# Sparse graph attention: 72 gathered chunks in place of 75 per sweep, and the second block's first rows fetched earlier

## The chip, the cores and the metric

The kernel runs on one core of a Trainium2 chip. The metric is the device time of one execution in microseconds, from the first to the last instruction. The profile is of one such execution.

## The reference

Four layers are applied to `x` of shape (16 graphs, 1024 nodes, 128 features), all with the same adjacency matrix `adj` (1024 x 1024, an entry is 1 with probability 1/128, so a node has about eight neighbours). Layers L0, L2 and L3 are attention layers with eight heads of 16; L1 is a graph attention layer. Cut to what matters:

```
def attention_layer(adj, h):                       # L0, L2, L3
    Q, K, V = h @ Wq, h @ Wk, h @ Wv               # 8 heads of 16
    s = einsum('bnhd,bmhd->bhnm', Q, K) / sqrt(16)
    a = softmax(where(adj == 0, -inf, s))          # over neighbours m
    x = layer_norm(h + einsum('bhnm,bmhd->bnhd', a, V) @ Wo + bo)
    return layer_norm(x + relu(x @ W1 + b1) @ W2 + b2)

def graph_layer(x, adj):                           # L1
    h = x @ W
    e = leaky_relu((h @ a_src)[:, :, None] + (h @ a_dst)[:, None, :])
    att = nan_to_num(softmax(where(adj == 0, -inf, e)))
    return layer_norm(att @ h + x)
```

All is in float32.

## The kernel before

**Sorting and slots.** `graph` counts each node's neighbours, ranks the nodes by degree, and cuts the ranking into 32 row groups of 32 nodes (T = 8 sorted rows of 128 nodes, J = 4 groups in each). A destination tile t is made of four groups j, one from each group column; `row_of(t, j)` says from which sorted row the group comes. `CAPS` says how many neighbours a group may have. For each sorted row, in the order `order`, the kernel fetches the adjacency rows by an indirect DMA (`by_position`) and finds the neighbours by rounds of max-of-eight and match-replace on DVE (L370 to L378). `slots` then makes, for each tile, the lists of neighbours (`idx`) and the 0/1 matrices (`marks`).

**Chunks.** A chunk (j, r) holds four slots (S = 4) for each of the 32 nodes of group j, so it fills 128 partitions. One indirect DMA on POOL's queue (L908) gathers the 128 rows of a chunk from a table of keys and values in DRAM. What remains over whole chunks of four is put together in one mixed chunk per tile (`MIX`), which serves two of the groups in halves of 64 partitions (`SHARED`). The chunks of a tile are cut into pieces of one or two (`PIECES`). With the mixed chunks there are 75 chunks in the eight tiles.

**Units and parts.** The 16 graphs are taken in two halves (`GR`, g). A unit is (layer, half, tile), so there are 64 units, eight for each half of each layer; these eight are called a sweep here, or a block in the title. The main loop runs over parts. In an attention layer a part is one piece; in L1 up to two pieces are one part. For a part, `products` (L920, DVE) multiplies the gathered keys with the queries, `exponentials` reduces them (L943, DVE) and takes the exponential (L947, ACT), `weighted` (L971, DVE) multiplies the values, and `summed` (L987, PE) sums over the slots by matmuls of `marks`, 32 output columns each, the output going to the PSUM partitions of group j. `gathered(i - 1 + AHEAD)` issues the gathers four parts ahead, into a ring of four buffers. In L1 there are no products with queries. `divided` closes a unit (the reciprocal at L1024).

**What lies between.** The order of instructions on every engine is written out by hand. Each part has three turns `others()` (four in L1), in which generators advance one step: the `tails` of the unit before (output projection, two layer norms, the feed-forward part, the projection for the next layer's tables, L543 to L731), then the first of `fronts` (slots of the next unit, input rows, weights, queries), then `loads`, then `slow`. `slow` is `at_leisure(1)`: during the first sweep of L0 it makes the tables of the second half of the graphs, in 16 steps of transposes (L617) and projections (L547). Before the first gather of the second sweep (u == T in `gathered`), all of `slow` that is left is advanced to its end. `loaded(u)` fetches the input rows of L0's units by indirect DMAs on POOL's queue (L827), in two halves h, and turns each with PE transposes (L617). [...]

Of the kernel before, what the change touches and what calls it, by code (L numbers as in the profile page):

```python
# [16 lines left out]
I32 = mybir.dt.int32  # L17
# [33 lines left out]

S = 4
J = P // 32
CAPS = (24, 14, 14) + 5 * (12,) + 8 * (10,) + 8 * (8,) + 6 * (6,) + 2 * (4,)
TOP = max(CAPS)
QUADS = TOP // S
MIX = J

def row_of(t, j):
    return T - 1 - t if j % 2 else t


def cap(t, j):
    return CAPS[row_of(t, j) * J + j]


COUNT = [[cap(t, j) // S for j in range(J)] for t in range(T)]  # L70

SHARED = [[j for j in range(J) if cap(t, j) % S] for t in range(T)]
assert all(len(_s) == 2 for _s in SHARED) and all(c % (S // 2) == 0 for c in CAPS)

PIECES = []
for _t in range(T):
    PIECES.append([])
    for _r in range(max(COUNT[_t])):
        for _p in range(2):
            _c = [(_j, _r) for _j in (_p, _p + 2) if COUNT[_t][_j] > _r]  # L80
            _last = PIECES[_t][-1] if PIECES[_t] else []
            if len(_c) == len(_last) == 1 and _c[0][0] == _last[0][0]:
                _last.extend(_c)
            elif _c:
                PIECES[_t].append(_c)
    PIECES[_t].insert(3, [(MIX, 0)])

PLACE = {
# [5 lines left out]
for _t in range(T):  # L94
    for _j in range(J):
        for _r in range(COUNT[_t][_j]):
            MARK[_t, _j, _r] = len(MARK)
    for _k in range(2):
        MARK[_t, MIX, _k] = len(MARK)


def of_piece(v, piece):
# [25 lines left out]
def sparse_path(ctx: ExitStack, tc: tile.TileContext, a: dict, out: bass.AP, flag):  # L128
# [87 lines left out]
    def graph(wide):  # L216
# [18 lines left out]
        nc.gpsimd.memset(lists, 0.0)  # L235
        for e in wide[3:] + wide[:1] + wide[2:3]:
            nc.gpsimd.memset(e, 0.0)
        caps = s1.tile([P, T], F32, name="caps")
        cols = s1.tile([P, 2, T], F32, name="cols")
        nid = s1.tile([P, T], F32, name="nid")  # L240

# [53 lines left out]
            yield 1  # L295

        rank_i = s1.tile([P, T], I32, name="rank_i")
        flip = s1.tile([P, T], I32, name="flip")
        nc.vector.tensor_copy(rank_i, rank)
        nc.vector.tensor_scalar(flip, rank_i, 32, None, ALU.bitwise_and)  # L300
        nc.vector.tensor_scalar(flip, flip, float((T - 1) * P // 32), None, ALU.mult)
        nc.vector.tensor_tensor(flip, rank_i, flip, ALU.bitwise_xor)
        where = s1.tile([P, T], F32, name="where")
        nc.vector.tensor_copy(where, flip)

        pack = s1.tile([P, T], F32, name="pack")
        nc.vector.tensor_scalar(pack, nid, -1.0, float(2 * N * N + N), ALU.mult, ALU.add)
# [34 lines left out]
                in_offset=bass.IndirectOffsetOnAxis(ap=node_i[:, q : q + 1], axis=0),  # L342
            ))

        order = [q for k in range(T // 2) for q in (k, T - 1 - k)]
        ahead = [by_position(q) for q in order[:3]]
        there = s1.tile([P, T], F32, name="there")
        for j in range(J):
            rows = slice(32 * j, 32 * j + 32)
            if j % 2 == 0:  # L350
                nc.vector.tensor_copy(there[rows], node[rows])
                continue
            for t in range(T):
                q = row_of(t, j)
                nc.vector.tensor_copy(there[rows, t : t + 1], node[rows, q : q + 1])
# [4 lines left out]
                    ALU.mult, ALU.add,  # L360
                )
        low = s1.tile([P, T], F32, name="low")
        nc.vector.tensor_tensor(bad, sorted_[:, :, 2], caps, ALU.is_gt)
        nc.vector.tensor_scalar(low, sorted_[:, :, 2], 1.0, None, ALU.is_lt)
        nc.vector.tensor_tensor(bad, bad, low, ALU.add)
        yield 2
# [1 line left out]
        for at, q in enumerate(order):  # L368
            v = vs[:, :N]
            nc.vector.scalar_tensor_tensor(v, ahead[at], 0.0, values, ALU.not_equal, ALU.mult)  # L370
            if at + 3 < T:
                ahead.append(by_position(order[at + 3]))
            top = -(-CAPS[q * J] // 8) * 8
            for k in range(0, top, 8):
                nc.vector.max(lists[:, q, k : k + 8], v)
                if k + 8 < top:
                    last, v = v, vs[:, N:] if k % 16 == 0 else vs[:, :N]
                    nc.vector.match_replace(v, lists[:, q, k : k + 8], last, 0.0)  # L378
                yield 1
            if 0 < at < 5:  # L380
                yield ("spread", "load", "slots", "queries")[at - 1]

    def slots():

        def spread(q):
            ps = bank([P, J, TOP])
            for j in range(J):
                nc.tensor.matmul(
                    ps[:, j, :], rep_of(j, True), lists[:, row_of(q, j), :],
                    start=True, stop=True,  # L390
                )
            return ps

        for q in range(T):
            ps = spread(q)
            yield
            if q:
                yield
            for s in range(S):
                at = slice(32 * s, 32 * s + 32)  # L400
                nc.vector.tensor_copy(
                    val[at], ps[at].rearrange("p j (k s) -> p j k s", s=S)[:, :, :, s]
                )

            first, second = SHARED[q]
            for k in range(2):
                at = slice(32 * (2 + k), 32 * (3 + k))
                to, of = COUNT[q][first], S * COUNT[q][second] + k
                nc.vector.tensor_copy(val[at, first, to : to + 1], ps[at, second, of : of + 1])

            def flat(v):
                return v.rearrange("p j k -> p (j k)")

            nc.vector.tensor_copy(flat(val_i), flat(val))

            for k, (by, op) in enumerate(
                ((2 * N - 1, ALU.bitwise_and), (11, ALU.logical_shift_right))
            ):
                nc.vector.tensor_scalar(flat(part), flat(val_i), by, None, op)
                nc.vector.tensor_scalar(  # L420
                    flat(idx[:, k, q]), flat(part), -1.0, float(N), ALU.mult, ALU.add
                )
            nc.vector.tensor_scalar(flat(used), flat(val), 0.0, None, ALU.is_gt)
            for j in range(J):
                c, n = MARK[q, j, 0], COUNT[q][j]
                nc.vector.tensor_tensor(
                    marks[:, c : c + n, :],
                    used[:, j, :n].rearrange("p (k o) -> p k o", o=1).to_broadcast([P, n, 32]),
                    mark32.to_broadcast([P, n, 32]),
                    ALU.mult,  # L430
                )
            for k in range(2):
                at, r = slice(64 * k, 64 * k + 64), COUNT[q][first]
                nc.vector.tensor_tensor(
                    marks[at, MARK[q, MIX, k], :],
                    used[at, first, r : r + 1].to_broadcast([64, 32]),
                    mark32[at, 0, :],
                    ALU.mult,
                )
            yield  # L440
# [410 lines left out]
    def queries(u):  # L851

        l, g, t = units[u]
        if not is_attention(u):
            ps = bank([P, J + 1, G])
            for j in range(J):
                nc.tensor.matmul(ps[:, j, :], rep_of(j, True), srcs[g, t], start=True, stop=True)
            for k, j in enumerate(SHARED[t]):
                at = slice(64 * k, 64 * k + 64)
                nc.tensor.matmul(  # L860
                    ps[at, MIX, :], rep_of(j, True)[:, at], srcs[g, t], start=True, stop=True
                )
            ofs[u] = smalls.tile([P, J + 1, G], F32, tag="of", name="of")
            nc.scalar.copy(ofs[u], ps)
            return
# [20 lines left out]
    def shared(u):  # L886

        qx[u] = queries_of_shared()
        for k, j in enumerate(SHARED[units[u][2]]):
            at = slice(64 * k, 64 * k + 64)  # L890
            nc.sync.dma_start(qx[u][at], qs[u][at, j, :])

    def gathered(i):
        if i >= len(parts):
# [1 line left out]
        u, pieces = parts[i]  # L896
        if u == T:
            while slow:
                advance(slow)
        l, g, t = units[u]  # L900
        width = tables[l, g].shape[1]
# [78 lines left out]
    def marked(t, chunk, outs, rhss):  # L980

        j, r = chunk
        for mark, j in (
            [(MARK[t, j, r], j)] if j < J else [(MARK[t, MIX, k], SHARED[t][k]) for k in range(2)]
        ):
            mine = [c for c in sum(PIECES[t], []) if c[0] == j or c[0] == MIX and j in SHARED[t]]
            nc.tensor.matmul(  # L987
                outs[32 * j : 32 * j + 32], marks[:, mark, :], rhss,
                start=(chunk == mine[0]), stop=(chunk == mine[-1]),
            )  # L990

    def summed(i):
# [3 lines left out]
        r = pieces[-1][-1][1]  # L996
        if is_attention(u) and i + 1 < len(parts) and pieces[-1][-1][0] != MIX:
            v, ((first, *_), *_) = parts[i + 1]
            if v == u and first[1] == r and first[0] != MIX:
                return  # L1000
        if u not in accums:
            accums[u] = accs.tile([P, HF, GH * D], F32, tag="acc", name="acc")
# [75 lines left out]
    with tc.manual_schedule():  # L1078
# [27 lines left out]
        prods = ctx.enter_context(tc.tile_pool(name="prods", bufs=4))  # L1106
        smalls = ctx.enter_context(tc.tile_pool(name="smalls", bufs=3))
        slow.append(at_leisure(1))
        for i in range(AHEAD - 1):
            gathered(i)  # L1110
        nc.gpsimd.memset(wide[3], 0.0)
        gathered(AHEAD - 1)
        fronts.extend([islice(rest, 3), loaded(1)] + more)
        closing, sizes = None, ()
        begun = 0
        for i in range(len(parts) + 2):
# [499 lines left out]
```

## Time and profile before

| what | value |
|---|---|
| median of 3 runs | 2327.65 us |
| lowest, highest | 2319.72, 2335.47 us |
| span of the profiled execution | 2318.9 us |
| PE busy | 2064.1 us (89%) |
| DVE busy | 1933.8 us (83%) |
| ACT busy | 1528.7 us (66%) |
| POOL busy | 1091.8 us (47%) |
| mean granted PE clock | 0.955 |
| moved by DMA | 636.05 MB |

A busy share is an average over stages with different limits. In what follows the span is cut at the reciprocals of L1024, one per unit, and each stretch is read by itself. In a row of the table of groups, the two numbers after the first bar are the busy time and the mean duration of one (ns), and after the second bar stands how long the engine was idle just before, with what ended most of it. In a timeline line the first number is the start, the second the time, both in us.

### The profile page before, as it was taken

How to read it: one execution, taken by the hardware profiler on the slowest of the kernel's cores; microseconds unless marked ns; L12 is line 12 of the kernel's file. 1: busy time of each engine (PE TensorE's matmuls, PEld its weight loads, DVE VectorE, ACT ScalarE, POOL GpSimd, SP SyncE). 2: the span in 40 equal slices, each digit the busy share in tenths (PEclk: the TensorE clock that was granted, in tenths of full speed). 3: DMA queues.
4: the chain of work that ended last, by engine and by line, in shares of the span. 5: the costliest groups of instructions: out<-in, count | busy, mean ns of one | idle time of the engine just before them, and what ended most of it. 6: DMA issues, size and time to landing. Idle time of an engine off the chain costs nothing. (4 is left out here: it accounts for less than half of the span.)

```text
span 2318.9 us, 36591 instructions
## 1 busy us (share of the span) xinstructions
PE 2064.1 (89%) x13124; PEld 1274.2 (55%) x13124; DVE 1933.8 (83%) x1486; ACT 1528.7 (66%) x5057; POOL 1091.8 (47%) x754
## 2 busy tenths in 40 slices
PE   7469999889998999997999989999999989898987
PEld 6326666555555555554565655655555555455554
DVE  7978788698889577778888899988898888988893
ACT  3227777767776655565576776787776767676764
POOL 3444435345454578883343434343354544544441
PEclk8779999999999999999899999999999999999988
DMA  7767878778787799997987978888887777676760
GB/s 265 243 232 259 291 275 284 273 249 294 267 295 267 235 329 354 345 367 268 326 289 275 320 269 290 285 316 290 284 282 272 255 268 281 231 270 242 269 246 21
DMA packets 168461, 636.05 MB, mean 274 GB/s; under 512 B 38328, under 2 KB 41144, under 8 KB 119774
## 3 DMA queue, kind: packets, MB, share of 16 engines
q0 software_dynamic: 92672, 485.09, 58.4%
q1 hardware_dynamic: 75600, 148.55, 19.0%
q8 instruction: 105, 1.72, 0.3%
q14 instruction: 84, 0.69, 0.1%
HBM read 603.11 MB, written 92.34 MB: 300 GB/s over the span
## 5 line engine op out<-in xcount | busy, mean ns | idle before, releaser
L908 POOL DMA_INDIRECT e<-table,idx x600 | 880.5, 1468 | 1029.6 <-DVE pr L971 834.7
L971 DVE TENSOR_TENSOR pr<-e,ex 128x2048 f32<-128x2048 f32 (+1 forms) x336 | 689.2, 2060 | 21.8 <-ACT ex L959 16.1
L920 DVE TENSOR_TENSOR pr<-e,qr 128x2048 f32<-128x2048 f32 x204 | 461.8, 2264 | 160.5 <-DMA e<-table,idx 88.9
L987 PE MATMUL acc<-pr,marks 128*32 128x512 f32 x2656 | 537.0, 615 | 38.2 <-DVE pr L971 28.3
L943 DVE TENSOR_REDUCE sc<-pr 128x128 f32<-128x2048 f32 (+1 forms) x252 | 518.5, 2058 | 8.6
L595 ACT ACTIVATE z<-yps,root 128x128 f32<-128x128 f32 x888 | 316.9, 387 | 35.7 <-PE yps L710 18.8
L987 PEld LDWEIGHTS acc<-pr,marks 128*32 128x32 f32 x2656 | 109.3, 111 | 291.1 <-issue 219.4
L706 PE MATMUL yps<-W,f 128*128 128x128 f32 x1520 | 251.7, 282 | 7.4 <-ACT f L701 0.7
L610 ACT ACTIVATE z<-yps,rstd 128x128 f32<-128x128 f32 x888 | 253.4, 368 | 7.2
L701 ACT ACTIVATE f<-ps,b 128x512 f32<-128x512 f32 x190 | 130.8, 692 | 157.4 <-PE ps L692 153.9
L706 PEld LDWEIGHTS yps<-W,f 128*128 128x128 f32 x1520 | 204.5, 191 | 48.8 <-issue 26.5
L547 PE MATMUL ps<-Wkv,xT 128*128 128x256 f32 x768 | 218.0, 426 | 12.7 <-ACT xT L623 4.3
L880 PE MATMUL ps<-q,rep 32*128 32x512 f32 x768 | 179.0, 656 | 47.3 <-ACT q L875 44.9
L883 ACT COPY qr<-ps 128x512 f32<-128x512 f32 x384 | 197.0, 599 | 31.7 <-PE ps L880 30.9
L947 ACT ACTIVATE ex<-sc 128x128 f32<-128x128 f32 (+1 forms) x252 | 78.6, 312 | 194.7 <-DVE sc L943 194.5
L617 PE MATMUL ps<-ident,z 128*128 128x128 f32 x896 | 175.6, 299 | 34.8 <-ACT z L610 29.9
L617 PEld LDWEIGHTS ps<-ident,z 128*128 128x128 f32 x896 | 114.6, 142 | 158.7 <-ACT z L610 85.8
L595 ACT ACTIVATION_READ_ACCUMULATOR z<-yps,root 128x1 f32 x888 | 201.3, 227 | 0.0
L551 ACT COPY kv<-ps 128x512 f32<-128x512 f32 x176 | 103.0, 590 | 136.7 <-PE ps L547 109.4
L547 PEld LDWEIGHTS ps<-Wkv,xT 128*128 128x128 f32 x768 | 149.8, 209 | 70.4 <-ACT qr L883 19.8
L692 PE MATMUL ps<-x,W 128*128 128x512 f32 x384 | 187.1, 610 | 0.9 <-ACT x L625 0.9
L681 PE MATMUL yps<-Wo,oT 128*128 128x128 f32 x768 | 159.2, 290 | 10.0 <-ACT oT L623 10.0
(173 smaller groups left out, 2724.3 us busy)
## 6 DMA issues: line engine op xcount, KB each, us to landing
table<-kv SPq DMA_DIRECT2D x88, 512.0 KB
qx<-qr SPq DMA_DIRECT2D x96, 256.0 KB
kept<-xT SPq DMA_DIRECT2D x96, 256.0 KB
x<-kept SPq DMA_DIRECT2D x48, 512.0 KB
e<-table,idx POOLq DMA_INDIRECT x600
table<-kv SPq DMA_DIRECT2D x32, 256.0 KB
edges<-in_adj SPq DMA_DIRECT2D x8, 512.0 KB
spare<-in_x SPq DMA_DIRECT2D x8, 512.0 KB
```

Of the source, the lines that this page charges most:

```text
L547: nc.tensor.matmul(ps[:, k, :], x[:, i + k, :], w[LAYERS[l][0], "Wkv"], start=True, stop=True,)
L595: nc.scalar.activation(z[:, i, :], y[:, i, :], AF.Square, scale=D**-0.5, bias=root, accum_out=total[:, i : i + 1],)
L610: nc.scalar.activation(z[:, i, :], y[:, i, :], AF.Copy, scale=rstd[:, i : i + 1])
L617: nc.tensor.transpose(ps[:, i, :], z[:, i, :], ident)
L692: nc.tensor.matmul(ps, p["W1"][:, f * P : (f + 1) * P], x1.rearrange("p g n -> p (g n)"), start=True, stop=True,)
L706: nc.tensor.matmul(ps[:, i, :], f1[:, f, i * P : (i + 1) * P], p["W2"][:, f, :], start=(f == 0), stop=False,)
L883: nc.scalar.copy(qs[u][:, j, h * GH * D : (h + 1) * GH * D], pss[j])
L908: nc.gpsimd.indirect_dma_start(out=es[i][:, k, :], out_offset=None, in_=tables[l, g][:, :], in_offset=bass.IndirectOffsetOnAxis(ap=idx[:, ...
L920: nc.vector.tensor_tensor(prs[i][0][:, :n, :], es[i][:, :n, :ROW], qx[u].rearrange("p (o c) -> p o c", o=1) if (MIX, 0) in piece else of_p ...
L943: nc.vector.tensor_reduce(sc[:, :n, :], prs[i][0][:, :n, :].rearrange("p k (a d) -> p k a d", d=HD), mybir.AxisListType.X, ALU.add,)
L971: nc.vector.tensor_tensor(prs[i][k0 // 2][:, :m, :].rearrange("p k (a d) -> p k a d", d=d), es[i][:, k0 : k0 + m, base : base + ROW].rearr ...
L987: nc.tensor.matmul(outs[32 * j : 32 * j + 32], marks[:, mark, :], rhss, start=(chunk == mine[0]), stop=(chunk == mine[-1]),)
```

## The change

Slots are counted in ones. `CAPS` and `row_of` become hand-set tables: for each tile four capacities, and for each group column the order of the sorted rows. What is over in each group, now 0 to 3 slots, fills quarters of 32 partitions of the mixed chunk (`QUARTERS`), so that up to three groups share it. The pieces are made by taking the chunks two at a time. There are 72 chunks: tile 0 has 11 in place of 12, tile 7 has 7 in place of 9, the others have 9 as before. In `graph`, a node's place is looked up from its rank by a compare with 32 group numbers and a sum of `MOVES`, in place of a bit flip; the rows are searched in another order, and the steps of the first slots, the loading and the first queries are yielded in another order. `shared` copies quarters. In `gathered`, when `slow` is driven to its end before the second sweep, tails that hold buffers are advanced first. In `summed`, no more than two parts are summed together. Last, the generator `loaded(1)` is started before the first gathers, so that its first fetch of rows stands ahead of them on POOL's queue.

```diff
-CAPS = (24, 14, 14) + 5 * (12,) + 8 * (10,) + 8 * (8,) + 6 * (6,) + 2 * (4,)
+ROWS = (
+    (0, 1, 2, 3, 4, 5, 7, 6),
+    (7, 6, 3, 5, 2, 1, 0, 4),
+    (7, 6, 5, 1, 2, 0, 3, 4),
+    (1, 0, 2, 3, 4, 7, 5, 6),
+)
+CAPS = (
+    (24, 5, 4, 11), (12, 6, 6, 12), (10, 9, 8, 9), (9, 8, 11, 8),
+    (8, 10, 10, 8), (7, 12, 13, 4), (5, 14, 9, 8), (6, 8, 8, 6),
+)
...
 PIECES = []
 for _t in range(T):
-    PIECES.append([])
-    for _r in range(max(COUNT[_t])):
-        for _p in range(2):
...
+    _c = [(_j, _r) for _r in range(QUADS) for _j in (0, 2, 1, 3) if COUNT[_t][_j] > _r]
+    PIECES.append([sorted(_c[_k : _k + 2]) for _k in range(0, len(_c), 2)])
     PIECES[_t].insert(3, [(MIX, 0)])
...
-        nc.vector.tensor_scalar(flip, rank_i, 32, None, ALU.bitwise_and)
-        nc.vector.tensor_scalar(flip, flip, float((T - 1) * P // 32), None, ALU.mult)
-        nc.vector.tensor_tensor(flip, rank_i, flip, ALU.bitwise_xor)
+        nc.vector.tensor_scalar(rank_i, rank_i, 5, None, ALU.logical_shift_right)
+        nc.vector.tensor_copy(ranks, rank_i)
+        which = junk[:, : T * T * J].rearrange("p (t k) -> p t k", t=T)
+        nc.vector.tensor_tensor(
+            which,
+            ranks.rearrange("p (t o) -> p t o", o=1).to_broadcast([P, T, T * J]),
+            iota[:, : T * J].rearrange("p (o k) -> p o k", o=1).to_broadcast([P, T, T * J]),
+            ALU.is_equal,
+        )
...
-        order = [q for k in range(T // 2) for q in (k, T - 1 - k)]
+        order = sorted({row_of(0, j) for j in range(J)})
+        order += [q for q in range(T) if q not in order]
...
             if 0 < at < 5:
-                yield ("spread", "load", "slots", "queries")[at - 1]
+                yield ("load", "spread", "queries", "slots")[at - 1]
...
         if u == T:
             while slow:
+                while busy[0] and not held[0]:
+                    advance(tails)
                 advance(slow)
...
-            if v == u and first[1] == r and first[0] != MIX:
+            if v == u and first[1] == r and first[0] != MIX and i - 1 not in prs:
                 return
...
         slow.append(at_leisure(1))
+        second = loaded(1)
+        next(second)
         for i in range(AHEAD - 1):
             gathered(i)
         nc.gpsimd.memset(wide[3], 0.0)
         gathered(AHEAD - 1)
-        fronts.extend([islice(rest, 3), loaded(1)] + more)
+        fronts.extend([islice(rest, 3), second] + more)
```

## The prediction

> **What bounds the kernel now.** First the totals, then the table of operation groups, then the stretches between the reciprocals at L1024. There is one reciprocal per unit (eight destination tiles of a layer and half of the graphs), so a stretch between two of them is about one unit.
>
> ```profile
> PE 2064.1 (89%) x13124; PEld 1274.2 (55%) x13124; DVE 1933.8 (83%) x1486; ACT 1528.7 (66%) x5057; POOL 1091.8 (47%) x754
> ```
> PE and DVE are both nearly full; over the whole span neither stands out as the bound.
>
> ```profile
> L908 POOL DMA_INDIRECT e<-table,idx x600 | 880.5, 1468 | 1029.6 <-DVE pr L971 834.7
> L987 PE MATMUL acc<-pr,marks 128*32 128x512 f32 x2656 | 537.0, 615 | 38.2 <-DVE pr L971 28.3
> L943 DVE TENSOR_REDUCE sc<-pr 128x128 f32<-128x2048 f32 x198 | 452.6, 2286 | 6.8
> L943 DVE TENSOR_REDUCE sc<-pr 128x64 f32<-128x1024 f32 x54 | 65.9, 1220 | 1.8
> L971 DVE TENSOR_TENSOR pr<-e,ex 128x1024 f32<-128x1024 f32 x72 | 87.9, 1221 | 2.9 <-issue 2.9
> L920 DVE TENSOR_TENSOR pr<-e,qr 128x2048 f32<-128x2048 f32 x198 | 454.4, 2295 | 160.5 <-DMA e<-table,idx 88.9 <-PE acc L987 46.1 <-issue 8.0
> ```
> In an attention layer a piece of two chunks costs DVE 2.295 + 2.286 + 2.288 = 6.87 us (product, reduce, weighting); a piece of one chunk costs 1.22 × 3 = 3.66 us. The gathers are no bound: POOL mostly waits for DVE to free a buffer.
>
> The stretches, in order: two of the first block (layer L0, first half of the graphs), an ordinary unit of L2, a unit 0 of L2, and an L1 unit 0 with the unit after it. Columns: length; busy PE, PEld, DVE, ACT, POOL; PE clock; DMA.
>
> ```profile
> core 0: us, PE busy (x) PEld busy (x) DVE busy (x) ACT busy (x) POOL busy (x), PEclk, DMA share, GB/s
> 213.20:254.90 41.70, 39.44 (x263) 26.03 (x260) 35.46 (x37) 31.13 (x104) 16.92 (x12) 1.00 0.78 275
> 420.00:465.90 45.90, 39.64 (x264) 26.14 (x262) 32.39 (x18) 32.63 (x111) 15.25 (x10) 1.00 0.69 250
> 1233.30:1269.70 36.40, 34.08 (x223) 21.57 (x223) 32.16 (x19) 27.63 (x89) 14.31 (x10) 1.00 0.87 296
> 1379.80:1423.40 43.60, 38.56 (x242) 22.61 (x244) 42.45 (x26) 28.99 (x92) 19.51 (x13) 1.00 0.75 261
> 923.10:945.60 22.50, 21.63 (x133) 11.18 (x131) 16.31 (x22) 10.63 (x41) 18.98 (x14) 1.00 0.88 291
> 945.60:964.20 18.60, 16.47 (x127) 10.09 (x126) 12.62 (x18) 10.26 (x40) 15.68 (x12) 1.00 0.98 364
> ```
> The limits differ by unit. Unit 0 (12 chunks) is bound by DVE: 42.45 of 43.60 us. An ordinary unit of 9 chunks has PE at 34.08 and DVE at 32.16 of 36.40; both have a few microseconds of slack. L0's first block is bound by PE (39.44 of 41.70), because it also projects the other half of the graphs. L1's units move data almost all the time (DMA share 0.98).
>
> **The first unit**, by the timeline from the first gather on:
>
> ```profile
> 84.85 1.18 POOL L908 DMA_INDIRECT e<-table,idx  x1 [3.47 <-issue]
> 97.25 2.29 DVE L920 TENSOR_TENSOR pr<-e,qr 128x2048 f32<-128x2048 f32 x1 [3.35 <-DMA e<-table,idx]
> 100.72 0.96 POOL L827 DMA_INDIRECT rows<-in_x,places  x1 [0.30 <-issue]
> 108.75 1.09 PE L617 MATMUL ps<-ident,rows 128*128 128x128 f32 x4 [20.29 <-DMA rows<-in_x,places]
> 116.66 2.89 POOL L827 DMA_INDIRECT rows<-in_x,places  x1 [0.30 <-issue]
> 125.89 1.09 PE L617 MATMUL ps<-ident,rows 128*128 128x128 f32 x4 [3.49 <-DMA rows<-in_x,places]
> 159.65 0.77 DVE L401 COPY little<-ps 32x24 f32<-32x24 f32 x4 [8.20 <-PE ps L388]
> ```
> PE stood 20.29 us for the first half of unit 1's input rows, which POOL issued after seven gathers. But DVE works nearly throughout: between 97.25 and the reciprocal at 169.8 it is busy 60.4 of 72.5 us, and its own waits there are 3.4 (first gather), 2.7 (L493 for PE L488) and 8.2 (L401 for PE L388). Those 14.3 us are all that a better start could give DVE.
>
> [...] 2656 records of 615 ns are 1633 us of durations in 537 us of busy time, a factor of 3.0. [...] Here PE got the rows 8.0 us after their issue (100.72 to 108.75)[...].
>
> **Part 1: three chunks fewer.** By the slot tables unit 0 goes from 12 to 11 chunks (seven pieces to six; a one-chunk piece goes) and unit 7 from 9 to 7 (five pieces to four; a two-chunk piece goes). Units 1 to 6 keep nine chunks. This happens in 2 halves × 4 layers. DVE work removed in the six attention sweeps: 6 × (3.66 + 6.87) = 63.2 us, and two weightings in each of L1's two sweeps, 2 × (2.29 + 1.22) = 7.0: together 70.2 us. How much of it shows:
> - Unit 0, attention. DVE-bound, so all 3.6 us count: 38.8 us of DVE remain, above PE (38.56 less one chunk). A chunk on PE is (38.56 − 34.08)/3 = 1.49 us. Five such units outside the first block: −18.0. Bounds per unit: 2.5 to 3.7.
> - Unit 7, attention. DVE falls to 25.3 us and stops counting. PE falls by 2 × 1.49 to 31.1; with the 2.4 us of PE idle kept, 36.4 becomes 33.5: −3.0. Bounds: 0 (the chain of its tail sets it) and 4.8 (PE leaves 0.6 us idle). Four such units: −12.0. The very last unit has the same piece less ahead of its end: −3.5 (0 to 6.9).
> - L1: (22.50 − about 17.4 for the units around)/3 = 1.7 us a chunk, as DMA and PE share the bound; three chunks, two sweeps, give 10; I take −8, because the units next to the layer's ends overlap attention work.
> - Marks. Units 2 and 6 now share their mixed chunk among three row groups, not two: one more mark matmul each (L987 falls only from 1328 to 1312 matmuls). [...] 0 to 1.49 us a unit, taken as 0.25; 16 units: +4.
> - Queries of the mixed chunk go in 108 copies rather than 96, with the same bytes: SP adds 12 issues of about 0.55 us on an engine that waits most of the time; nothing. ACT loses 12 exponentials, POOL 24 gathers; both hidden, since neither is a bound.
>
> **Part 2: the start.**
> - The map from rank to place: five operations of 0.2 us become three such, two of 256 elements (nearest row, L451 128x256, 0.42), a reduce (L449, 0.41) and an add: about 2.0 against 1.0, +1.0 on the path. The 14 additional one-column copies at 0.07 lie under the 3.5 us wait for the first gathered edges.
> - Unit 0's slots need five searched rows (0, 1, 7, 2, 3) and not four: six more operations of 1.24 us, so the indices are ready at 77.4 + 1.0 + 7.5 = 85.9. The first gather started at 84.85, held by the table's writes, so it moves by about +1.5. The search as a whole has the same 26 operations.
> - The first half's rows of unit 1 now go out while POOL waits for those indices: the issue costs nothing, and the 20.29 us wait is gone.
> - The second half's rows still follow the gathers that wait for the first weighting. Before, that weighting ended at 112.0 and PE had the rows at 125.9. PE now meets this transpose ahead of the first sums (eight L987 matmuls, 3.6 us) and of L488, for which DVE's L493 waits. Rows at about 127.4, L488 done at about 133; DVE is ready at about 124.4: a wait of 8.6 in place of 2.7, +5.9. In exchange L388 no longer sits behind a row transpose: −8.2. With unit 0's piece: 1.5 + 5.9 − 8.2 − 3.7 = −4.5.
> - Unit 0 has one piece and so three filler turns fewer, so unit 2's two halves are turned back to back in unit 1. PE waits for the second, again behind gathers: 4 to 10 us, less what such waits cost there before; taken as +5.
> - One projection step of the other half moves from unit 0 to unit 7, where all that is left is forced out before the second block's first gather: 1.1 + 3.8 = 4.9 us of PE in a PE-bound stretch, against −3.0 for its two chunks: +2.
> - Sum of the first block: +2.5; bounds −11 and +15.
>
> **Sum:** −18.0 − 12.0 − 3.5 − 8 + 4 + 2.5 = −35.0 us on the span of 2318.9, hence 2283.9. The three runs have a median of 2327.65, 8.7 above that span; so 2292.6, taken as 2292. About 1% (23 us) is what a measurement of this kernel can tell from no change.
>
> **The rivals.**
> - *DVE sets the time throughout.* All 70.2 us count and the start gives its 11 us: 2327.65 − 81 = 2246. For it: DVE at 88% even in ordinary units, and POOL's 834.7 us of waiting for DVE. Against: PE at 34.08 of 36.40 in those units. Chance 0.15.
> - *Unit 7 gives nothing*, since its tail steps and the next queries, which have to fit in four pieces, become the chain. Then −18.0 − 3.4 (L1's unit 0) + 4 + 2.5 = −15: 2313. For it: ordinary units take 36.4 with either engine short of full. Chance 0.22.
> - *PE's granted clock falls.* It is 0.955 in the mean, with stretches at 0.91 where PE is at 36.3 of 36.4 us. If denser PE work lowers it, each 0.01 costs 2064 × 0.01/0.955 = 21.6 us; from 0.016 on the gain is gone, and 0.03 would give 2327.65 − 35 + 65 = 2358. Against: the stretches at 0.91 took no longer than the others, so not every dip reaches the end. Chance 0.10.
> - That the change doesn't do what it says is excluded by the instruction order: 576 gathers against 600, and one row fetch ahead of them.
>
> **How the numbers follow.** The forecast has 0.53; its own range is 2268 to 2312. Faster by over 1% (under 2304): 0.44 of the forecast, all 0.15 of the first rival, 0.04 of the second, 0.63. Within 1%: 0.09 + 0.17 + 0.01 = 0.27. Slower: 0.10. The range runs from the middle of the first rival to above the second, leaving the clock's case out: 2252 to 2322.
>
> **What would show it.** Right: DVE near 1864 us busy; attention unit 0 near 40 us and unit 7 near 33.5, with PE above 90% there; no PE wait of 20 us near 90 us, but one ahead of the first L987 sums; the first block's eighth reciprocal within 10 us of 465.9. Wrong: unit 7 still at 36 (second rival) or near 30 (first), units 2 and 6 longer by over 1 us, or a mean clock under 0.94.

## The result, and the profile after

The changed kernel takes 2301.26 us (median of four runs, 2297.37 to 2309.91) against 2323.68 us for the kernel before beside it: a ratio of 0.990, 95% interval 0.9852 to 0.9949, or 22 us less (12 to 34). The forecast was 2292 us, 35 us less, with a range of 2268 to 2312. The profiled span fell from 2318.9 to 2299.1 us, with a mean clock of 0.952 (0.955 before).

The totals of the changed kernel, and its rows of gathers, weightings, products and sums in the table of groups:

```profile
PE 2052.0 (89%) x13140; PEld 1270.4 (55%) x13140; DVE 1873.9 (82%) x1472; ACT 1529.9 (67%) x5041; POOL 1043.7 (45%) x730
...
L941 POOL DMA_INDIRECT e<-table,idx x576 | 834.9, 1449 | 1034.6 <-DVE pr L1004 804.2
L1004 DVE TENSOR_TENSOR pr<-e,ex 128x2048 f32<-128x2048 f32 (+1 forms) x320 | 661.2, 2075 | 52.3 <-ACT ex L980 28.5
L953 DVE TENSOR_TENSOR pr<-e,qr 128x2048 f32<-128x2048 f32 x192 | 440.1, 2292 | 151.0 <-DMA e<-table,idx 85.1
L1020 PE MATMUL acc<-pr,marks 128*32 128x512 f32 x2624 | 534.7, 623 | 14.5 <-DVE pr L1004 11.4
```

There are 576 gathers instead of 600, and 192 products of two chunks instead of 198. DVE is busy 59.9 us less, where 70.2 were worked out for the chunks; 3.5 of the difference is one copy at the start (last section), 2.9 the marks that are now made by quarters, and 1.0 the lookup. The chunks are gone, and the span fell by 19.8. The data is not gone:

```profile
DMA packets 165197, 636.06 MB, mean 277 GB/s; under 512 B 35064, under 2 KB 37880, under 8 KB 116510
```

The kernel before moves 636.05 MB; on POOL's queue, with the gathers and the other indirect transfers, 485.09 MB before and 485.08 after. In the code a slot without a neighbour has an index out of bounds, and these figures show that it brings no data. What was saved are empty slots: work of the engines, and no transfer.

The stretches between reciprocals of the changed kernel, with the columns as before: the second, third and eighth unit of the first block; unit 7 of L0 and unit 0 of L1 at the edge between these layers; then in L2 an ordinary unit, a unit 7 and the unit 0 behind it.

```profile
core 0: us, PE busy (x) PEld busy (x) DVE busy (x) ACT busy (x) POOL busy (x), PEclk, DMA share, GB/s
167.40:217.90 50.50, 44.20 (x270) 30.24 (x270) 36.08 (x40) 31.54 (x102) 13.90 (x12) 0.86 0.65 227
217.90:262.80 44.90, 42.61 (x272) 28.57 (x266) 35.57 (x39) 31.65 (x104) 16.44 (x12) 0.92 0.80 286
428.60:474.70 46.10, 39.86 (x246) 27.34 (x247) 25.76 (x15) 30.74 (x98) 17.02 (x12) 0.93 0.63 230
741.30:773.90 32.60, 28.31 (x169) 19.59 (x167) 19.90 (x19) 20.95 (x81) 16.09 (x15) 0.84 0.72 239
773.90:811.20 37.30, 33.97 (x207) 19.05 (x207) 15.31 (x18) 19.98 (x78) 11.27 (x12) 0.95 0.67 211
1232.70:1268.90 36.20, 34.13 (x223) 21.56 (x223) 32.15 (x19) 27.58 (x89) 14.18 (x10) 1.00 0.88 307
1341.80:1375.60 33.80, 30.04 (x191) 18.66 (x190) 25.77 (x16) 24.81 (x81) 14.98 (x10) 0.95 0.73 252
1375.60:1417.00 41.40, 37.84 (x232) 21.82 (x231) 39.00 (x21) 28.43 (x92) 16.88 (x10) 1.00 0.78 273
```

Unit 0 of L2 went from 43.6 to 41.4 us, with DVE at 39.0 where 38.8 was worked out. Unit 7 takes 33.8 us where 33.5 was worked out, with DVE down to 25.77; the ordinary unit is unchanged. Unit 2 of the first block took 41.7 us before and takes 44.9 at a clock of 0.92.

The start of the first unit of the changed kernel, by the timeline:

```profile
86.69 0.95 POOL L851 DMA_INDIRECT rows<-in_x,places  x1 [0.30 <-issue]
91.68 1.02 POOL L941 DMA_INDIRECT e<-table,idx  x1 [4.03 <-DVE little L447]
101.75 1.09 PE L641 MATMUL ps<-ident,rows 128*128 128x128 f32 x4
102.51 2.29 DVE L953 TENSOR_TENSOR pr<-e,qr 128x2048 f32<-128x2048 f32 x1 [2.12 <-DMA e<-table,idx]
115.36 2.28 DVE L1004 TENSOR_TENSOR pr<-e,ex 128x2048 f32<-128x2048 f32 x1
122.08 2.28 DVE L1004 TENSOR_TENSOR pr<-e,ex 128x2048 f32<-128x2048 f32 x1
122.31 2.89 POOL L851 DMA_INDIRECT rows<-in_x,places  x1 [0.31 <-issue]
129.37 1.09 PE L641 MATMUL ps<-ident,rows 128*128 128x128 f32 x4 [10.50 <-DMA rows<-in_x,places]
130.39 3.41 PE L1020 MATMUL acc<-pr,marks 128*32 128x512 f32 x16
134.37 0.16 DVE L517 TENSOR_TENSOR b<-b,ps 128x2 f32<-128x2 f32 x1 [5.99 <-PE ps L512]
156.83 0.76 DVE L422 COPY little<-ps 32x24 f32<-32x24 f32 x4
169.34 1.09 PE L641 MATMUL ps<-ident,rows 128*128 128x128 f32 x4 [5.80 <-DMA rows<-in_x,places]
```

The first fetch stands ahead of the gathers, and its transpose at 101.75 waits for nothing: the wait of 20.29 us is gone. But the transpose of the second half waits 10.50 us. The first sums start only behind it, at 130.39, though the first two weightings ended at 117.64 and 124.36, and DVE's L517 waits 5.99 us for PE's L512 after them. The wait of 8.20 us at the copy that is now L422 is gone. A new wait of 5.80 us, for unit 2's second half, follows at 169.34. The prediction names all of these. The late first gather (91.68 in place of 84.85) was foreseen only to 1.5 us of the 6.8.

### The profile page after: what moved, and what is told of

Read it like the earlier page. It is cut to its first block, busy times and chain, and to the rows that moved or that the text cites. A ratio compares the mean times of both kernels' runs of the same rounds, so it can differ in the third digit from the quotient of the medians.

```text
span 2299.1 us, 36570 instructions
## 1 busy us (share of the span) xinstructions
PE 2052.0 (89%) x13140; PEld 1270.4 (55%) x13140; DVE 1873.9 (82%) x1472; ACT 1529.9 (67%) x5041; POOL 1043.7 (45%) x730
## 2 busy tenths in 40 slices
DMA packets 165197, 636.06 MB, mean 277 GB/s; under 512 B 35064, under 2 KB 37880, under 8 KB 116510
## 3 DMA queue, kind: packets, MB, share of 16 engines
q0 software_dynamic: 89216, 485.08, 59.1%
## 5 line engine op out<-in xcount | busy, mean ns | idle before, releaser
L941 POOL DMA_INDIRECT e<-table,idx x576 | 834.9, 1449 | 1034.6 <-DVE pr L1004 804.2
L1004 DVE TENSOR_TENSOR pr<-e,ex 128x2048 f32<-128x2048 f32 (+1 forms) x320 | 661.2, 2075 | 52.3 <-ACT ex L980 28.5
L953 DVE TENSOR_TENSOR pr<-e,qr 128x2048 f32<-128x2048 f32 x192 | 440.1, 2292 | 151.0 <-DMA e<-table,idx 85.1
L976 DVE TENSOR_REDUCE sc<-pr 128x128 f32<-128x2048 f32 (+1 forms) x240 | 497.4, 2073 | 8.1
L619 ACT ACTIVATE z<-yps,root 128x128 f32<-128x128 f32 x888 | 319.0, 389 | 34.9 <-PE yps L734 16.1
L571 PE MATMUL ps<-Wkv,xT 128*128 128x256 f32 x768 | 209.7, 412 | 22.8 <-ACT xT L647 16.4
L907 ACT COPY qr<-ps 128x512 f32<-128x512 f32 x384 | 197.4, 602 | 41.8 <-PE ps L904 41.7
L716 PE MATMUL ps<-x,W 128*128 128x512 f32 x384 | 192.4, 625 | 12.5 <-ACT x L649 12.4
L904 PE MATMUL ps<-q,rep 32*128 32x512 f32 x768 | 169.1, 648 | 37.0 <-ACT q L899 35.0
L571 PEld LDWEIGHTS ps<-Wkv,xT 128*128 128x128 f32 x768 | 144.2, 201 | 75.4 <-ACT xT L647 19.4
```

The lines of the kernel that those rows point to most:

```text
L571: nc.tensor.matmul(ps[:, k, :], x[:, i + k, :], w[LAYERS[l][0], "Wkv"], start=True, stop=True,)
L619: nc.scalar.activation(z[:, i, :], y[:, i, :], AF.Square, scale=D**-0.5, bias=root, accum_out=total[:, i : i + 1],)
L716: nc.tensor.matmul(ps, p["W1"][:, f * P : (f + 1) * P], x1.rearrange("p g n -> p (g n)"), start=True, stop=True,)
L907: nc.scalar.copy(qs[u][:, j, h * GH * D : (h + 1) * GH * D], pss[j])
L941: nc.gpsimd.indirect_dma_start(out=es[i][:, k, :], out_offset=None, in_=tables[l, g][:, :], in_offset=bass.IndirectOffsetOnAxis(ap=idx[:, ...
L953: nc.vector.tensor_tensor(prs[i][0][:, :n, :], es[i][:, :n, :ROW], qx[u].rearrange("p (o c) -> p o c", o=1) if (MIX, 0) in piece else of_p ...
```

## The experiments

Every ratio is against the kernel before, run beside it. "Eighth reciprocal" is the end of the first block in the profiled execution: 465.9 us before, 474.7 after.

**Without the early fetch.** From the changed kernel:

```diff
-        second = loaded(1)
-        next(second)
-        fronts.extend([islice(rest, 3), second] + more)
+        fronts.extend([islice(rest, 3), loaded(1)] + more)
```

> The changed kernel, with unit 1's first rows fetched after the first gathers again. Theory (the gain is the three chunks; the early fetch only moves PE's wait from the first half of the rows to the second, ahead of the first sums): within 5 us of the changed kernel, so 2296 to 2307 us; PE's wait for the first half (near 20 us) returns, the first unit ends within 4 us of 167.4. Rival (the early fetch is a gain that something else hides): slower than the changed kernel by 8 us or more, near 2310 or above.

Measured: 2296.82 us, 0.9862 (0.9832 to 0.9891); eighth reciprocal at 469.0. The whole gain is there without the fetch. The first unit ends at 159.8 and not within 4 us of 167.4, so this part of the expectation failed: from the first product to the first reciprocal it takes 61.0 us here, 64.9 in the changed kernel and 72.5 in the kernel before. The early fetch lengthens this stretch, and the wait of 8.20 us, which the prediction sets against the cost of the fetch, is gone without it too.

**The early fetch alone.** The kernel before with the lines that the last diff takes out.

> The kernel before, with the early fetch alone and its 75 chunks. Theory: no measurable difference from the kernel before, ratio 0.997 to 1.003; PE's first wait of 20 us is gone and a wait for the second half of the rows stands ahead of the first sums. Rival (the early fetch carries the gain): 10 to 20 us faster than the kernel before, ratio 0.991 to 0.996.

Measured: 2321.45 us, 0.9984 (0.9967 to 1.0002); eighth reciprocal at 468.8. Moving PE's longest wait away is worth at most 0.3%: in its place PE waits 10.58 us for the second half. The wait at the copy (L401 there) fell from 8.2 to 1.9 us and the one of L493 rose from 2.7 to 6.0: the queue of gathers only holds up the second half now.

**All of the change, but 75 chunks.** Tiles 0 and 7 get their chunks back:

```diff
-    (24, 5, 4, 11), ...
+    (24, 9, 4, 11), ...
-    ... (6, 8, 8, 6),
+    ... (10, 8, 8, 10),
```

> The changed kernel with tile 0 at 12 and tile 7 at 9 chunks, 75 in all; everything else of the change stays, and two more search operations come into the setup. Theory: it loses what units 0 and 7 gained (16 + 15 us in the two traces) and keeps what the first block lost (9 us), so 8 to 12 us slower than the kernel before, near 2332. Rival (the gain comes from the new order of pieces and setup, not from the chunks): within 5 us of the changed kernel, near 2303.

Measured: 2336.17 us, 1.0037 (1.0023 to 1.0051), 9 us more than before. Its stretches for the first block's unit 7, and for a unit 7 and a unit 0 of L2:

```profile
430.20:476.90 46.70, 40.01 (x268) 26.64 (x267) 32.46 (x19) 32.55 (x111) 13.20 (x10) 1.00 0.60 215
...
1357.00:1393.60 36.60, 34.41 (x223) 21.69 (x226) 32.29 (x20) 27.48 (x88) 14.17 (x10) 1.00 0.75 256
1393.60:1440.10 46.50, 42.87 (x244) 24.68 (x244) 42.45 (x25) 28.85 (x90) 17.69 (x13) 0.93 0.70 250
```

DVE is back at 42.45 us in unit 0, and unit 7 at 36.6. So the gain is the three chunks, and the rest of the change costs something. (This kernel also searches two more times during the setup.)

**Unit 7 with nine chunks, unit 0 with eleven.** Only tile 7's line is changed, to (10, 8, 8, 10): 74 chunks.

> The changed kernel with tile 7 at 9 chunks (74 in all), so that only unit 0's chunk is saved. Theory: it loses unit 7's gains of L2 and L3 and the end (2.8 + 3.9 + 4.0 + 3.2), but not those of L0, where unit 7 lies in stretches that PE and ACT set: 12 to 18 us slower than the changed kernel. Rival (unit 7's chunks are worth their DVE time everywhere, 6.9 us in six sweeps): 35 us or more slower. Rival 2 (unit 7 gives nothing): within 5 us.

Measured: 2326.84 us, 0.998 (0.9963 to 0.9997). The same three stretches of this kernel:

```profile
425.90:481.10 55.20, 45.98 (x280) 30.96 (x279) 32.43 (x18) 34.74 (x114) 13.86 (x10) 0.94 0.58 210
1353.50:1390.20 36.70, 36.58 (x220) 23.31 (x220) 32.17 (x19) 26.92 (x87) 13.10 (x10) 0.91 0.79 284
1390.20:1430.20 40.00, 35.94 (x219) 20.43 (x219) 38.93 (x22) 26.54 (x87) 19.67 (x12) 1.00 0.74 257
```

Unit 0 falls by itself (40.0 us, DVE 38.93) while unit 7 stays at 36.7: two gains that the two edits tell apart. They aren't wholly independent: unit 0 takes 41.4 us in the changed kernel, behind a unit 7 of seven chunks, and 40.0 here, behind one of nine. In the first block unit 7 shows what it hides: 46.7 us with nine chunks and twelve in unit 0, 55.2 with nine and eleven, 46.1 with seven and eleven. With a piece less in unit 0 this stretch gets 8.5 us longer, and unit 7's two chunks give 9.1 back. By the code the longer stretch is the projection step that moves there.

**The changed kernel again**, beside the last, as its yardstick.

> The changed kernel itself once more, as the measure for the three others. Theory: 2295 to 2303 us, ratio to the kernel before 0.986 to 0.992. In its first profile four copies of the constant rep took 3.5 us longer than in five other profiles, before anything that the change touches; if that was chance, the first product lies near 99 us and not at 102.5. Rival (the longer copies belong to the change): 102 again.

Measured: 2308.64 us, 0.9917 (0.9888 to 0.9946); eighth reciprocal at 472.6. Unit 7's two chunks are worth 2326.84 − 2308.64 = 18 us.

**One more mark.** Every mixed chunk gets one more group, whose 0/1 matrix is zero (64 units, not 16):

```diff
+for _s in SHARED:
+    _s.append(min(set(range(J)) - set(_s)))
```

> The changed kernel with one mark matmul more for every mixed chunk, of zeros and into a PSUM group that the tile's mixed chunk doesn't use (64 units, 256 more matmuls of 512 columns as recorded). Theory (it runs beside the others, 0.25 us a unit): 5 to 20 us slower than the changed kernel. Rival (a mark costs what a chunk costs PE, 1.49 us a unit): 60 to 95 us slower. Third mark free: within 3 us.

Measured: 2312.15 us, 0.9936 (0.9907 to 0.9965), 3.5 us more than the changed kernel beside it, less than the intervals are wide. 384 more matmul records than in that kernel leave PE's busy time at 2058.2 us, between the 2052.0 and 2062.4 of the changed kernel's two traces. So a mark for a row group that the chunk doesn't use costs nothing that can be told from zero.

**Both halves of units 1 and 2 fetched at once.**

```diff
         rows = fetch(0)
+        early = fetch(1) if u in (1, 2) else None
...
-        rows = fetch(1)
+        rows = early or fetch(1)
```

> The changed kernel with both halves of the rows of units 1 and 2 fetched in one step. Theory (the waits of 10.5 us ahead of the first sums and of 5.8 us ahead of unit 2's queries are what the first block lost): both waits are gone, DVE's wait of 6.0 us for the bias and of 6.6 us for the sums with them, and the time is 8 to 12 us under the changed kernel, near 2291; the third reciprocal lies 8 us or more ahead of 262.8. Rival (the loss of the first block lies in the later search and slots): within 3 us of the changed kernel.

Measured: 2297.41 us, 0.9877 (0.9847 to 0.9907); eighth reciprocal at 465.1. Units 1 and 2 of this kernel:

```profile
163.90:206.90 43.00, 38.65 (x258) 25.20 (x258) 35.77 (x40) 30.82 (x101) 15.96 (x12) 1.00 0.74 264
206.90:251.50 44.60, 42.55 (x272) 28.25 (x266) 35.61 (x39) 31.66 (x104) 16.15 (x12) 0.92 0.81 288
```

Unit 1 loses its 7.5 us (50.5 to 43.0), and PE is 5.55 us less busy there with 12 matmul records fewer, at a clock of 1.00 in place of 0.86. The wait at 169.34 is gone. It cost twice in the changed kernel: PE stood for 5.80 us, and then ran at a lower clock (0.50 from 168 to 180 us; from 168 to 176 it is 1.00 in this kernel). The first unit ends 3.5 us earlier as well, but so much is already in the copies at the start (last section), which are 3.5 us shorter in this kernel. Its second fetch waits 6.91 us on POOL's queue, until 90.74, and the first gather behind it still starts at 92.00 (91.68 in the changed kernel). Unit 2 keeps its 44.6. The 8 to 12 us that were expected against the changed kernel aren't shown, as the intervals overlap.

**Slots ahead of the queries too.** The last kernel, with unit 0's slots yielded before its queries, and unit 1's second half in another buffer:

```diff
-                yield ("load", "spread", "queries", "slots")[at - 1]
+                yield ("load", "spread", "slots", "queries")[at - 1]
...
+                elif u == 1 and h:
+                    rows = hidden()[:, : GH * D].rearrange("p (g d) -> p g d", d=D)
```

> The changed kernel with both halves of unit 1's and unit 2's rows fetched early, the second half into another buffer, and the first slots made after three searched rows and not five. Theory (the first block's loss is the late indices and the two row waits): first product near 95 us, PE's wait ahead of the first sums gone, third reciprocal 12 us or more ahead of the changed kernel's, and 8 to 14 us faster than it. Rival (L0 is bound by PE's whole work, and time gained at the start is given back at the eighth unit): within 4 us of the changed kernel.

Measured: 2303.53 us, 0.9882 (0.9853 to 0.9911). The first product starts at 104.95 us and not near 95: that expectation failed. It is later than in the last kernel (103.51), but this kernel has the long copies of the last section, 3.5 us, and that one hasn't. Without them the new order would be some 2 us earlier (an estimate, 103.51 + 3.5 − 104.95).

**Unit 2 alone.** Without the early fetch of unit 1, but with both halves of unit 2 together (the edit before, for u == 2).

> The changed kernel with unit 1's rows fetched as in the kernel before (after the first gathers) and unit 2's two halves in one step. Theory (the first block's losses are the wait that the early fetch puts ahead of the first sums, and the second half of unit 2's rows): the first reciprocal near 160 as without the early fetch, the second near 205, and 5 to 10 us faster than the changed kernel, ratio to the kernel before 0.983 to 0.989. Rival (time gained ahead of the eighth unit is given back there): equal to the changed kernel within 3 us.

Measured: 2300.41 us, 0.9885 (0.9856 to 0.9913). Units 0 and 1 end at 209.3 us together (206.9 in the kernel with both fetched early, 217.9 in the changed one), and the eighth reciprocal is at 466.1.

**Three chunks less in L1 alone.** The kernel before with the last piece of tiles 0 and 7 left out in L1; it leaves out those neighbours there, and L0, L2 and L3 are as before.

```diff
+FEWER = [_pieces[:-1] if _t in (0, T - 1) else _pieces for _t, _pieces in enumerate(PIECES)]
...
-        todo = list(PIECES[t])
+        todo = list(pieces_of(u))
```

> The kernel before with three chunks left out in L1 alone: tile 0's last one-chunk piece and tile 7's last two-chunk piece are not gathered, weighted or summed there, so some neighbours are missing in L1. Theory after the result (where L1 meets the attention layers, its units are bound by the tails of attention units on PE and ACT, so fewer parts save nothing there): 0 to 4 us faster than the kernel before. Prediction's term (1.7 us a chunk): 8 to 10 us faster. Rival (fewer turns for the tails make the edge longer): slower by up to 4 us.

Measured: 2325.09 us, 0.999 (0.9972 to 1.0008): 2 us, with an interval from 6.5 less to 2 more. The 8 us that I had put down for L1 lie just outside it, though L1 is 7.3 us shorter in its one trace. The neighbours left out are data too: this kernel moves 634.17 MB, 1.88 MB less than before. At the 331 GB/s that L1 has in the trace of before these would take 5.7 us (an estimate), so here a shorter L1 need not come from the chunks alone. Its first block, whose work is that of the kernel before, ended at 475.4 us and not at 465.9; unit 2 of it, and six microseconds near that unit's beginning:

```profile
218.20:262.70 44.50, 42.37 (x263) 28.44 (x260) 35.22 (x37) 31.65 (x104) 16.47 (x12) 0.92 0.74 257
...
219.00:225.00 6.00, 5.97 (x20) 4.47 (x21) 5.96 (x5) 3.83 (x10) 1.39 (x2) 0.50 0.60 196
```

**Three chunks less in all layers.** The same piece left out everywhere (neighbours are left out in all four layers), and the changed kernel's two lines that advance tails when `slow` is driven to its end.

> The kernel before with the same three chunks left out in all layers, and tails that hold buffers advanced first where the second sweep begins; nothing else of the change, and some neighbours are missing. Theory (the chunks alone give 16 us in unit 0, 12 in unit 7, 3 at the end, and the rest of the change costs 9 to 12): 26 to 33 us faster than the kernel before, ratio 0.986 to 0.989, so faster than the changed kernel. Rival (the other parts of the change cost nothing): equal to the changed kernel within 3 us.

Measured: 2288.74 us, 0.9845 (0.9817 to 0.9873), 36 us less. A unit 7 and a unit 0 of L2 in it:

```profile
1325.40:1359.20 33.80, 30.14 (x191) 18.52 (x190) 25.76 (x17) 24.77 (x82) 14.97 (x10) 0.95 0.65 225
1359.20:1400.40 41.20, 37.60 (x243) 22.84 (x242) 38.94 (x22) 28.92 (x94) 16.87 (x10) 1.00 0.87 301
```

These are the changed kernel's own figures to 0.2 us, out of the old chunks. Leaving these chunks out is worth 36 us, more than the 26 to 33 expected, where the changed kernel has 19 to 22. But these chunks held neighbours: 622.94 MB are moved, 13.1 MB less than in either of the two kernels, so the 36 us aren't the price of the chunks alone.

**The kernel before again**, to see how much one trace of the first block is worth.

> The kernel before, unchanged, once more. If the first block's eighth reciprocal at 465.9 us is what the old start always gives, the changed kernel's 474.7 is a cost of the change, and it comes here at 464 to 468, with unit 2's stretch at 41.7. If the half-clock spells of PE fall differently in each execution (the same start in the kernel with three chunks less in L1 gave 475.4), it comes anywhere between 464 and 477, with unit 2 at 41.7 without a spell and near 44.7 with one. Ratio to the kernel before: 1.000, within 0.3%.

Measured: 2328.38 us, 0.9995 (0.9978 to 1.0012); eighth reciprocal at 469.0, unit 2 at 41.7.

## Why the forecast held, and where it did not

**The attention units: near the prediction in sum.** From trace to trace the five attention units 0 outside the first block give 0.2 + 7.9 + 2.2 + 2.0 + 3.7 = 16.0 us (18.0 predicted), the four units 7 give 1.3 + 2.8 + 3.9 + 4.0 = 12.0 (12.0), and the last unit 3.2 (3.5). In the trace of its repetition they give 11.8, 9.8 and 4.8, and two traces of the kernel before differ by 0.9, 2.1 and 1.7 in the same sums. The 74-chunk kernel tells the two gains apart. "DVE throughout" falls: unit 7 has 6.4 us less of DVE than with nine chunks (32.17 to 25.77) and gained about 3. "Unit 7 gives nothing" falls too. That the 16.0 are so near to 18.0 is partly luck: the bounds were 2.5 to 3.7 us for each unit, and four of the five lie outside them. L0's unit 0 gave only 0.2. PE is busy 40.64 of its 44.5 us and DVE 38.99, and behind a unit 7 of nine chunks it takes 40.9, so it seems to work off what unit 7 left over. L2's first gave 7.9, twice its price; it follows L1 and had 42.17 us of DVE in 46.6 before, and 38.39 in 38.7 after.

**L1: the term that was mis-sized.** "I take −8, because the units next to the layer's ends overlap attention work." By the sums of the stretches L1 changed by −1.1 us in the changed kernel's trace, and by +5.5 in that of its repetition. The same edge before (unit 7 of L0, unit 0 of L1):

```profile
731.50:765.40 33.90, 28.64 (x194) 17.89 (x194) 26.40 (x22) 22.39 (x87) 19.69 (x14) 1.00 0.76 246
765.40:800.30 34.90, 32.30 (x213) 18.82 (x211) 17.02 (x22) 20.44 (x80) 18.64 (x16) 1.00 0.74 232
```

Unit 0 of L1 is longer in the changed kernel: 34.9 before, 37.3 after. DVE is busy 15 of those 37.3 us. Its two longest waits there and in the unit behind, in the kernel before and then in the changed one (in all, times, longest):

```profile
DVE pr L971 <- ACT ex L959: 13.1, 2, 10.1
DVE both L1024 <- PE ps L567: 4.7, 1, 4.7
```

```profile
DVE pr L1004 <- ACT ex L992: 15.2, 3, 6.0
DVE both L1057 <- PE ps L1020: 10.1, 1, 10.1
```

DVE waits for exponentials in both; the wait of 10.1 us for PE's sums is new in this length (1.7 before). In the code the tails of L0's last unit advance in turns that belong to parts; with a part less there are fewer turns, and what is left over runs in L1, ahead of those sums. The 75-chunk kernel, which has the turns, takes 34.8 us at this place, and 16.6 for the unit after it (16.8 before). With eleven chunks in unit 0 and nine in unit 7 the two units are 4.0 us longer together, in the changed kernel 4.3. With the old chunks and a piece left out in L1 alone they are 2.5 us longer, though unit 0 is shorter there (32.3). That the two units together lengthen with fewer chunks is shown; that the missing turns are the reason is read from code and waits. In the changed kernel's trace the edge takes 4.3 of the 5.4 us that L1's other units give. I had sized the overlap at 2.

The edge isn't the whole of it. The 75-chunk kernel has the old edge, and yet its L1 is 6.2 us longer than before in its one trace: something else in the change may cost time in L1, though two traces of one kernel differ by 6.6 us there. And the term was priced on a bound that "DMA and PE share", while the chunks that go bring no data, so DMA had no less to do. In the kernel that leaves data out in L1, L1 is 7.3 us shorter. How much of the missing 7 us each of these makes is open.

**The first block: +2.5 predicted, +8.8 in the trace, and not separable from the scatter.** The trace's own sum, as the change in each term (predicted in brackets): first product 5.3 later (predicted 1.5); from there to the first reciprocal −7.6 (−6.0); unit 1 +7.0 (+5); unit 2 +3.2 (nothing predicted); unit 7 +0.1 (+2, out of 8.5 and −9.1 where I had 4.9 and −3.0: right in sum, wrong in both); the other units +0.8. Of the 5.3 at the start, 3.5 come from copies that run ahead of the steps that the change touches, as the last section shows. The other surprise is unit 2. The changed kernel and the kernel before, in slices around a short gap of PE near that unit's beginning:

```profile
216.00:219.00 3.00, 1.38 (x7) 0.55 (x8) 2.93 (x3) 1.80 (x10) 0.86 (x1) 0.96 0.26 88
219.00:225.00 6.00, 6.00 (x22) 4.50 (x23) 5.97 (x5) 3.83 (x10) 1.11 (x2) 0.50 0.85 289
```

```profile
211.00:214.00 3.00, 1.49 (x10) 0.47 (x8) 2.93 (x3) 1.76 (x10) 0.53 (x1) 1.00 0.29 100
214.00:220.00 6.00, 5.78 (x41) 4.67 (x44) 5.96 (x5) 4.34 (x13) 1.44 (x2) 1.00 0.59 190
```

PE is idle for about half of three microseconds in both; then it runs 22 matmuls in 6 us at a clock of 0.50 in one, and 41 at 1.00 in the other. Six microseconds at half clock (a spell) lose three (an estimate from these clocks), which is nearly the whole +3.2. The spell doesn't need the change: the kernel with three chunks less in L1 does the work of the kernel before up to there and has the same spell (20 matmuls in 6 us, clock 0.50), and the changed kernel's repetition has none (unit 2 at 42.1, clock 1.00). But the change may make it likelier. The clock of unit 2 is below 1.00 in eight of the nine traces that begin like the changed kernel or a variant of it, and in one of the five that begin like the kernel before or a variant of it. Three traces of the old start put the eighth reciprocal at 465.9, 469.0 and 475.4; three of the changed one (the third with the added marks) at 474.7, 472.6 and 472.8. The means differ by 3.3 us, near the +2.5, but by luck: all three of the changed kernels have the 3.5 us of copies, which the prediction hadn't. No single trace settles it. Only the 5.80 us wait in unit 1, with the lower clock behind it, is pinned by an edit: with both halves early it is gone, and unit 1 is at 43.0.

What starts a spell isn't shown. A gap of PE of 1.89 us was followed by a spell in the changed kernel, and a gap of 1.31 us in the kernel with three chunks less in L1; the same 1.31 us brought none in the kernel before.

**Marks: +4 predicted, about +1.** The 0.25 us a unit behind the +4 was the author's estimate. 3.5 us for 64 marks are 0.06 us a unit, 1 us for 16, and even that is not told from zero. In the changed kernel's trace the ten units 2 and 6 of the attention sweeps outside the first block are 2.0 us longer in all.

**The clock rival.** The mean went from 0.955 to 0.952; at the prediction's price of 21.6 us for 0.01 that is 6 us of the shortfall in this pair of traces. Over all runs it isn't excluded: the repetition of the changed kernel has a mean of 0.948 against 0.952 for the kernel before beside it, 9 us at that price; the kernel with both halves early has 0.951 against 0.953, the one without the early fetch 0.954 against 0.953. So a fall of up to 0.004 may be part of the shortfall. A fall to under 0.94, as the rival had it, didn't come.

**The sum.** Predicted −35.0; the trace has −19.8. L1 accounts for 7 of the difference and the first block for 6, the rest is small change either way. By the timed runs the changed kernel lies 13 to 17 us above the old chunks with a piece left out (2325 × (0.990 − 0.9845), and with 0.9917). The 13.1 MB that the latter doesn't fetch may be part of that, and 10.6 of the 16.6 us between their traces lie in the first block, 3.5 of them in the copies at the start. The L0 to L1 edge takes part in both (2.2 us there). What else the changed chunks cost is open: the lookup adds 1.0 us, the moved step is paid in both kernels' first block, and ordinary units of 36 to 38 us differ by 1 to 2 us either way in any two traces.

**A better version.** Without the early fetch 0.9862, with both halves early 0.9877, with unit 2's alone 0.9885: all below the changed kernel's 0.990 and 0.9917, with intervals that overlap its own. Their traces end the first block at 469.0, 465.1 and 466.1, but none of the three has the long copies. None is shown to be faster than the changed kernel.

## What to carry to other kernels

Price a chunk by the engine that bounds the unit it is taken from. Ask what it carried: the empty slots here cost engine time and no data (DVE is 59.9 us less busy without them, 636.06 MB are moved after 636.05), so where transfers are part of the bound, don't count on the chunk's whole share (−8 us predicted for L1, −1.1 in the trace). Ask also what its turns carried: where filler work advances with the chunks, fewer chunks leave it over, and it reappears at the next edge, as in the first block's unit 7 here (8.5 us longer with a piece less in unit 0). A long wait of an engine that isn't the bound can be worth little (PE's 20.29 us here: at most 0.3%), and moving its DMA ahead can move the wait to the next transfer (10.58 us for the second half). Before a few microseconds in one stretch are put down to an edit, look at the clock of that stretch and at a second trace of the old kernel (the same unit 2 took 41.7 us at a clock of 1.00 and 44.5 at 0.92).

## What was not expected of the hardware

The run-to-run spread goes with PE's granted clock. In the repeated kernel before, 22 runs between 2316.66 and 2342.14 us have mean clocks of 0.951 to 0.958, and a straight line through them falls by 2.5 us for each 0.001 (correlation −0.74), close to the prediction's 2.16. Which of the two brings the other isn't shown by this.

At the very start DVE makes four copies on 32 partitions, while POOL fills buffers. In the kernel before:

```profile
1.92 10.75 DVE L151 COPY rep<-ident 32x128 f32<-32x128 f32 x4
8.97 10.66 POOL L237 MEMSET e<- 128x4128 f32 x3
```

and in the changed kernel:

```profile
1.92 14.20 DVE L161 COPY rep<-ident 32x128 f32<-32x128 f32 x4
8.95 10.65 POOL L247 MEMSET e<- 128x4128 f32 x3
```

The third copy takes 3.8 us instead of 0.35. It does so in the changed kernel, its repetition, and the kernels with added marks and with slots ahead of the queries; in the others it is short. The changed kernel has it in both of its traces, the kernel before in neither. The traces point to what these copies wait for: in all fourteen, each of the four ends 0.07 to 0.15 us after an instruction of POOL does. In the kernel before the third ends at 9.11, behind a short fill that ends at 9.03, and the fourth at 12.67, behind the first of the long fills (12.59). In the changed kernel the third already comes in behind a long fill (12.56 after 12.48), and the fourth behind the next one (16.12 after 16.04). So one more fill, about 3.6 us, stands in DVE's way. The third copy and the fills around it start within 0.03 us of each other in the two kernels; why the order turns, and whether moving the fills would free DVE, wasn't tried.
